# Layer norm 1 of two batches on a transposed copy of x, instead of TensorE transposes

## The chip, the cores and the metric

The kernel runs on one NeuronCore of one Trainium2 chip. The metric is the device time of one execution in microseconds, the median over runs. TensorE (PE) multiplies matrices into PSUM, VectorE (DVE) and ScalarE (ACT) work on SBUF and PSUM, GpSimd (POOL) on SBUF, and SyncE (SP) issues most of the DMAs. Each engine takes its instructions in the order in which the program emits them.

## The reference

One cross attention block with an MLP, in float32, for B = 4 batches of 512 rows of width D = 512, with 16 heads of 32 and an inner width of 2048:

```python
x = layer_norm(hidden_states, ln1_w, ln1_b)
q = (x @ q_w + q_b).reshape(B, LQ, H, HD).transpose(0, 2, 1, 3)
k = (encoder_hidden_states @ k_w + k_b).reshape(B, LK, H, HD).transpose(0, 2, 1, 3)
v = (encoder_hidden_states @ v_w + v_b).reshape(B, LK, H, HD).transpose(0, 2, 1, 3)
scores = jnp.where(mask, jnp.einsum('bhqd,bhkd->bhqk', q, k) * scale, mask_value)
out = jnp.einsum('bhqk,bhkd->bhqd', jax.nn.softmax(scores, axis=-1), v)
hidden = out.transpose(0, 2, 1, 3).reshape(B, LQ, D) @ cproj_w + cproj_b + residual
y = jax.nn.gelu(layer_norm(hidden, ln2_w, ln2_b) @ fc_w + fc_b, approximate=True)
return hidden + y @ proj_w + proj_b
```

Layer norm 1 is `(x - mean) * rsqrt(var + eps) * w + b`, with mean and variance over the width of each row, and `w` and `b` along the width.

## The kernel before, in words

The attention of the four batches is cut into 16 groups of four heads (`w`, four per batch), and each group into two halves of 256 queries. A half is a block `p`, from 0 to 31: batch 0 has blocks 0 to 7, batch 1 has 8 to 15, and so on. `block` emits, in this order: the scores of eight head and query tiles on PE (`scores`, line 260, eight PSUM banks, which is all there are), the softmax of the first four (`soften`: one DVE step, line 266, and one ACT exponential, line 270), two of the next four, two 32 by 32 block transposes on DVE (`turn`, line 278), the last two softmaxes, and two more `turn`. Between these steps `fill` runs other work, listed for each block by `put`: the products `prep_k`, `prep_q`, `prep_v` of a later group (k4 is the k product of group 4, and so on), output projections (`cproj`), MLP products (`fc_by_pair`, `proj`), loads and norms. `CHAIN` is a planned cost of one product, and `fill(0)`, `fill(1)` take items up to that cost, `fill(2)` the rest.

After a block its probabilities are exchanged between partitions: `copies` emits four POOL copies (line 335) and twelve DMAs on SP (line 340) into `pT`, of which there is one buffer (`gt` and `xe` serve for some blocks). `attend` (line 357) of a block comes two to three blocks later, ahead of the scores of the block it is due in, and its result is scaled on DVE into `oT` (line 362). PSUM tiles are taken in turn from eight banks, so a tile waits for whoever reads the tile eight places before it.

Layer norm 1 of a batch: x is loaded with rows on partitions into four tiles `xn`; DVE takes mean and variance (`ln_stat`, lines 127 and 128); POOL makes the reciprocal root (`ln_rs`, line 135); ACT or DVE normalises (`ln_norm`, lines 145 and 149); PE transposes 16 tiles of 128 by 128 through the identity into four PSUM tiles `tp` (`ln_turn`, line 158); ACT or DVE moves each to `xT` with weight and bias (lines 163 and 161). For batch 1 the norm stands at the end of block 0's fill (ACT), and the turns in block 4 (all moved by ACT). For batch 3 statistics stand in blocks 13 and 15, the norms (DVE) in 15, the turns in 16 and 17 (two moves by ACT, two by DVE). All batches share one `xT`, so the last q product of a batch must be done before the next batch's `xT` is written. Queries of batch 1 are first needed by q4 in block 5, those of batch 3 by q12 in block 18.

`xn` is a pool of four buffers that also holds the residual tiles `h` of batch 1's rows 256 to 511 and others. The first two residual tiles of batch 1 are in the pool `hids` (six buffers). In block 17 `load_h` loads residual tiles of batch 1, `c_bias` adds a row to each on POOL (line 368), and `cproj` (line 397) multiplies on PE and adds into them on DVE (line 398). `fc_sums` makes weight sums of the MLP on POOL (lines 469 and 472), and `y_sums` makes sums of the normed rows `yT` (tile `ys`), for batch 0 two on DVE and two on POOL, behind the k product of block 11.

Of the kernel before, what the change touches and what calls it, by code (L numbers as in the profile page):

```python
# [12 lines left out]
F32 = mybir.dt.float32  # L13
# [7 lines left out]
P = 128  # L21
# [16 lines left out]

BY_ACT = ((1, 1), (1, 2))
NORM_ACT = BY_ACT + ((2, 0), (2, 1))  # L40
# [9 lines left out]
@with_exitstack  # L50
def xattn_block(ctx: ExitStack, tc: tile.TileContext, x, encT, mask, q_w, k_w, v_w, c_w, fc_w, p_w, vecs, rows, out):
    nc = tc.nc
# [4 lines left out]

    const, keep, hids, tiles, small = pools(ctx, const=1, keep=1, hids=6, tiles=4, small=4)
    dram = ctx.enter_context(tc.tile_pool(name="dram", bufs=1, space=bass.MemoryType.DRAM))
# [9 lines left out]
    m8 = one.tile([P, L], U8, tag="m8", name="m8")  # L69
    nhalf = const.tile([P, NT], F32, tag="nhalf", name="nhalf")  # L70
    qb = const.tile([P, NG], F32, tag="qb", name="qb")
    wc = one.tile([P, ND, D], F32, tag="wc", name="wc")
# [57 lines left out]
    def ln_rs(key):  # L130

        ve = small.tile([P, NT], F32, tag="ve", name=f"ve{key[0]}_{key[1]}")
        nc.gpsimd.tensor_scalar(ve, S["mv", key][:, :, 1], EPS, 1.0, ALU.add, ALU.mult)
        rs = small.tile([P, NT], F32, tag="rs", name=f"rs{key[0]}_{key[1]}")
        nc.gpsimd.tensor_tensor(rs, ve, nhalf, ALU.pow)
# [143 lines left out]

    def block(w, half, fill, pairs):  # L280

# [88 lines left out]
    def stays(b, t):  # L370

        return b == 0 or b == SPLIT and t < 2

    def load_h(b, *ts_):

        if ("xa", b) not in S:
            S["xa", b] = dram.tile([L, D], F32, tag=f"xa{b}", name=f"xa{b}")
        for t in ts_:
            if b == B - 1:

                S["h", b, t] = k_q(t // 2, t % 2)
            else:
                pool, tag = (hids, "hid") if stays(b, t) else (tiles, "xn")
                S["h", b, t] = pool.tile([P, D], F32, tag=tag, name=f"h_{b}_{t}")
            Q[0].dma_start(out=S["h", b, t], in_=x[b, ts(t, P), :])
            if stays(b, t):
                S["hid", b, t] = S["h", b, t]
# [456 lines left out]
    def do(fn):  # L844
        return [(0.0, fn)]

    def A(w):
        if w >= NW:
# [32 lines left out]
    make_identity(nc, ident)  # L881
    nc.gpsimd.memset(nhalf, -0.5)
    load_enc(0)
    load_w(0, nc.sync, ("wv",))
# [17 lines left out]
    prep_k(1)  # L902
    run(turns1(0))
    load_h(0, *range(NT))
    nc.sync.dma_start(out=wc, in_=c_w)
# [7 lines left out]
    v_bias(0)  # L913

    def norm1(b, *ts_):
        for t in ts_:
            S["xn", b][t] = tiles.tile([P, D], F32, tag="xn", name=f"xn1_{b}_{t}")
            ln_norm((1, b), t, S["xn", b][t], gt[:, ts(t, D)])

    S["xn", 1] = [None] * NT  # L920
    x3 = turns1(1)


# [33 lines left out]

    ahead, fills = {}, {}

    def put(p, *work, before=()):  # L960

        work = [item for part in work for item in part]
        ahead[p] = list(before)
        fills[p] = work
# [22 lines left out]
    k, q, v = A(9)  # L987
    put(11, [k], do(lambda: y_sums(0)), [v], some(2), pb_(0))

# [33 lines left out]
    for p in range(2 * NW):  # L1023
# [10 lines left out]

        block(w, half, fill, any(cost > CHAIN for cost, _ in fills[p]))

# [61 lines left out]
```

## Time and profile before

| | us |
|---|---|
| median of 3 runs | 769.5 |
| lowest, highest | 768.61, 769.65 |
| the profiled execution | 768.29 |
| its span | 766.5 |

The span is from the first to the last instruction of the program; the rest of the profiled execution's time, 1.8 us, lies around it. The profile's page gives busy times by engine, the chain of work that ended last, and groups of instructions by source line; queries of the trace give timelines (start, length, engine, line, operation, operands, count, and in brackets the idle time before it and what ended it), waits, and busy time in chosen stretches. Times in timelines are microseconds from the start of the span. A float32 matmul stands as two records, a transpose as one. The recorded end of a matmul is modelled and overlaps the next start, so the cost of a matmul on PE is read from start to start.

### The profile page before, as it was taken

Reading aid. Unit: us, or ns where it says so; the run is one execution under the profiler, and the core shown is the slowest. Engines: PE = TensorE matmul, PEld = TensorE weight load, DVE = VectorE, ACT = ScalarE, POOL = GpSimd, SP = SyncE. Lnnn points to the kernel's source line nnn. Section 1 sums busy time; section 2 is a strip of 40 time slices with the busy share of each in tenths; the row PEclk is TensorE's granted clock in tenths of the full one; section 3 lists DMA queues with packets and bytes.
Section 4 is the critical chain, followed back from the end, with each engine's and each line's share of the span. In section 5 each row is a group of like instructions: output and inputs, shape, how many; then the busy total and the mean of one; then the engine's idle time right before and its main releaser. Section 6 shows DMA issues by size and latency. Waiting matters only on the chain.

```text
span 766.5 us, 13025 instructions
## 1 busy us (share of the span) xinstructions
PE 760.6 (99%) x4474; PEld 520.1 (68%) x4474; DVE 594.7 (78%) x1188; ACT 337.1 (44%) x761; POOL 312.6 (41%) x330
## 2 busy tenths in 40 slices
PE   9999999999999999999999999999999999999998
PEld 7656555566754745565554566447888889988997
DVE  3889899878989757887888989855777886747862
ACT  2676766564776444737753567501202221021200
POOL 1525447369466374234575444530060014303152
PEclk9999999999999999999999999999999999999999
DMA  9978788466866766675656866793724412146001
GB/s 330 319 223 228 180 209 253 117 196 193 254 196 189 189 208 180 163 185 130 173 128 190 214 197 193 173 296 132 262 101 129 162 34 90 35 131 219 2 15 42
DMA packets 58721, 131.44 MB, mean 171 GB/s; under 512 B 10992, under 2 KB 16752, under 8 KB 58528
## 3 DMA queue, kind: packets, MB, share of 16 engines
q1 hardware_dynamic: 56592, 123.58, 56.2%
q0 software_dynamic: 1920, 7.01, 2.7%
q8 instruction: 36, 0.59, 0.3%
q14 instruction: 29, 0.24, 0.1%
q10 hardware_dynamic: 144, 0.02, 0.0%
HBM read 66.08 MB, written 11.01 MB: 101 GB/s over the span
## 4 chain that ended last, share of the span: by engine, by line
PE 98%; DVE 1%; POOL 0%; ACT 0%; issue 0%; POOLq 0%
PE q L518 25%; PE accp L578 11%; PE r L665 8%; PE sc L260 8%; PE av L357 8%; PE accq L229 7%; PE accc L397 7%; PE accv L240 7%; PE acck L217 7%; PE q4p L701 2%; PE q1p L719 2%; PE tp L158 2%; PE warm L891 1%; DVE ptt L266 0%; PE q3p L701 0%; PE q5p L701 0%
## 5 line engine op out<-in xcount | busy, mean ns | idle before, releaser
L270 ACT ACTIVATE ptt<-ptt,mn 128x512 f32<-128x512 f32 x256 | 181.6, 711 | 148.6 <-DVE mn L266 148.6
L266 DVE CUSTOM_DVE_ANT_0 ptt<-sc,mb 128x512 f32<-128x512 f32 x256 | 160.5, 682 | 19.2 <-PE sc L260 19.2
L278 DVE STREAM_TRANSPOSE tb<-ptt 128x1024 f32<-128x1024 f32 x128 | 153.5, 1217 | 0.3 <-ACT ptt L270 0.2
L335 POOL COPY pT<-tb 32x1088 f32<-32x1088 f32 x96 | 105.2, 1096 | 38.1 <-DVE oT L362 14.4
L578 PE MATMUL accp<-pbt,gt 128*128 128x512 f32 x192 | 84.9, 596 | 0.0
L518 PE MATMUL q<-yT,gt 128*128 128x256 f32 x320 | 78.9, 380 | 0.0
L539 ACT ACTIVATE ga<-ga,vec 128x512 f32<-128x512 f32 x40 | 26.7, 714 | 92.0 <-DVE ga L472 92.0
L578 PEld LDWEIGHTS accp<-pbt,gt 128*128 128x128 f32 x192 | 35.9, 190 | 45.8 <-issue 39.3
L518 PEld LDWEIGHTS q<-yT,gt 128*128 128x128 f32 x320 | 60.9, 190 | 8.6 <-DMA xa<-pbt 0.2
L260 PE MATMUL sc<-pbt 32*128 32x512 f32 x512 | 64.7, 614 | 0.0
L240 PEld LDWEIGHTS accv<-ptt,xe 128*128 128x128 f32 x512 | 59.1, 192 | 7.4 <-DVE mn L266 4.9
L518 PE MATMUL q<-ys,gt 128*128 128x256 f32 x240 | 61.6, 380 | 0.0
L240 PE MATMUL accv<-ptt,xe 128*128 128x128 f32 x512 | 60.0, 276 | 0.0
L217 PE MATMUL acck<-xe,ptt 128*128 128x512 f32 x128 | 58.9, 603 | 0.0
L229 PE MATMUL accq<-xe,ptt 128*128 128x512 f32 (+1 forms) x136 | 58.3, 574 | 0.0
L397 PE MATMUL accc<-wc,oT 128*128 128x512 f32 x128 | 56.4, 597 | 0.0
L472 DVE TENSOR_TENSOR ga<-q,ga 128x512 f32<-128x512 f32 (+1 forms) x60 | 36.2, 603 | 21.4 <-PE q L518 19.4
L518 PEld LDWEIGHTS q<-ys,gt 128*128 128x128 f32 x240 | 45.7, 190 | 6.1
L270 ACT ACTIVATION_READ_ACCUMULATOR ptt<-ptt,mn 128x1 f32 x256 | 47.8, 187 | 0.0
L252 POOL TENSOR_TENSOR v<-v,row 128x512 f32<-128x512 f32 x16 | 20.4, 1280 | 64.7 <-ACT v L245 64.3
L357 PE MATMUL av<-pT,v 128*32 128x256 f32 x768 | 46.4, 382 | 0.0
L229 PEld LDWEIGHTS accq<-xe,ptt 128*128 128x128 f32 x136 | 25.1, 190 | 30.7 <-issue 23.1
(181 smaller groups left out, 1163.4 us busy)
## 6 DMA issues: line engine op xcount, KB each, us to landing
pT<-tb SPq DMA_DIRECT2D x288, 136.0 KB, 2.4
pbt<-p_w_dram SPq DMA_DIRECT2D x40, 256.0 KB, 3.3
gt<-ws SPq DMA_DIRECT2D x20, 512.0 KB, 3.4
gt<-tb SPq DMA_DIRECT2D x48, 136.0 KB, 2.4
xe<-tb SPq DMA_DIRECT2D x48, 136.0 KB, 2.4
pbt<-fc_w_dram SPq DMA_DIRECT2D x24, 256.0 KB, 4.1
gt<-fc_w_dram SPq DMA_DIRECT2D x20, 256.0 KB, 3.4
ptt<-k_w_dram SPq DMA_DIRECT2D x16, 256.0 KB, 3.7
```

The source lines that it names most:

```text
L217: nc.tensor.matmul(acc, S["wk", w][:, d, :], eT[:, d, :], start=(d == 0), stop=(d == ND - 1))
L229: nc.tensor.matmul(acc, S["wq", w][:, d, :], xT[:, d, c], start=(d == 0), stop=(d == ND - 1))
L240: nc.tensor.matmul(acc[:, ts(t, P)], eT[:, d, ts(t, P)], S["wv", w][:, d, :], start=(d == 0), stop=(d == ND - 1),)
L260: nc.tensor.matmul(S["sc", w, qt][h], qT[r, ts(qt, P)], kT[r, :], start=True, stop=True)
L266: nc.vector.tensor_tensor_reduce(out=s, in0=S["sc", w, qt][h], in1=S["mb", w // NG], scale=1.0, scalar=FMAX, op0=ALU.add, op1=ALU.min, acc ...
L270: nc.scalar.activation(s, s, AF.Exp, bias=mn, scale=-1.0, accum_out=S["sums", w][:, qt, h : h + 1])
L278: nc.vector.transpose(tv[:, qt % 2, 2 * k : 2 * k + 2], S["ps", w, qt, k])
L335: nc.gpsimd.tensor_copy(pT[ts(i, HD), i], tb[ts(i, HD), i])
L357: nc.tensor.matmul(av[ts(h, HD), : 2 * P].rearrange(shape, **kw), v[:, t, ts(h, HD)], p[t][h], start=(t == 0), stop=(t == NT - 1),)
L397: nc.tensor.matmul(acc, S["oT", b][:, g, ts(t, P)], wc[:, g, :], start=(g == 0), stop=(g == NG - 1))
L518: nc.tensor.matmul(o, x[:, k], y[:, k], start=(k == 0), stop=(k == 1))
L578: nc.tensor.matmul(acc, gT[q % 2][:, k, ts(t, P)], S["pw", b, q * FQ + k], start=(k == 0), stop=(k == FQ - 1))
```

## The change

For batches 1 and 3 the turns on PE go away. The host hands over a second copy of x, `rawT`, with the width on partitions. The statistics are still taken from x with rows on partitions. POOL writes `rs` and `-mean * rs` into a tile `rn`; DVE transposes `rn` in blocks of 32 by 32 (`store_rn`); four small DMAs on SP write it to DRAM as two rows of 512; two DMAs read each row back to all 128 partitions (`load_rn`). `load_raw` loads four 256 KB tiles of `rawT` into the `xn` buffers. POOL multiplies each by the first row and adds the second (`ln1_rows`, eight instructions of 128 by 512 for a batch); ACT applies weight and bias into `xT` (`ln1_affine`, four instructions).

The diff also changes the order around it. For batch 1, `load_raw` is issued behind batch 0's turns and ahead of `load_h`, `wc` and the MLP weights; `store_rn` stands in block 0, `load_rn` in block 1, the POOL work half in block 1 and half in block 2, `ln1_affine` at the end of block 4. For batch 3, `load_raw` and `store_rn` stand in block 15 ahead of four MLP weight loads and the exchange of block 15, `load_rn` and all eight POOL instructions in block 16 ahead of `fc_sums` and the copies of block 16, `ln1_affine` in block 17. The rows' two tiles take two of the six `hids` buffers (tag `hid2`), which batch 1's first two residual tiles share, so their load moves from block 16 to block 17. And all of `y_sums(0)` now runs on DVE, at a new place `mid` of block 11, between the first four softmaxes and the next two.

```diff
-BY_ACT = ((1, 1), (1, 2))
+BY_ROW = ((1, 1), (1, 3))
+BY_ACT = ((1, 2),)
...
+        if key in BY_ROW:
+            rs, nm = rn[:, :NT], rn[:, NT : 2 * NT]
+            nc.gpsimd.tensor_tensor(rs, ve, nhalf, ALU.pow)
+            nc.gpsimd.tensor_tensor(nm, S["mv", key][:, :, 0], rs, ALU.mult)
+            nc.gpsimd.tensor_scalar(nm, nm, -1.0, 0.0, ALU.mult, ALU.add)
+            return
...
+    def load_raw(b):
+        S["xn", b] = [tiles.tile([P, L], F32, tag="xn", name=f"raw_{b}_{d}") for d in range(ND)]
+        for d in range(ND):
+            nc.sync.dma_start(out=S["xn", b][d], in_=rawT[b, ts(d, P), :])
+
+    def store_rn(b):
+        nc.vector.transpose(rnT, rn)
+        d = S["rn", b] = dram.tile([2, L], F32, tag=f"rn{b}", name=f"rn{b}")
+        for i in range(NI):
+            nc.sync.dma_start(
+                out=d.rearrange("a (t i q) -> i (a t) q", i=NI, q=HD)[i], in_=rnT[i * HD : i * HD + 2 * NT, :]
+            )
+
+    def load_rn(b):
+        S["rows", b] = [hids.tile([P, L], F32, tag="hid2", bufs=2, name=f"rn_{b}_{i}") for i in range(2)]
+        for i in range(2):
+            nc.sync.dma_start(out=S["rows", b][i], in_=S["rn", b][i : i + 1, :].broadcast_to([P, L]))
+
+    def ln1_rows(b, *ds):
+        for d in ds:
+            for i, op in enumerate((ALU.mult, ALU.add)):
+                nc.gpsimd.tensor_tensor(S["xn", b][d], S["xn", b][d], S["rows", b][i], op)
+
+    def ln1_affine(b):
+        for d in range(ND):
+            nc.scalar.activation(
+                xT[:, d, :], S["xn", b][d], AF.Identity,
+                bias=vec[:, LN1B + d : LN1B + d + 1], scale=vec[:, LN1W + d : LN1W + d + 1],
+            )
...
         soften(w, q0, 0, 1, 2, 3)
+        run(mid)
         soften(w, q1, 0, 1)
...
-        e = nc.vector if b > SPLIT else nc.gpsimd
+        e = nc.gpsimd if b == SPLIT else nc.vector
...
-    put(0, [(CHAIN, lambda: prep_v(1)), v2, k2], do(lambda: norm1(1, *range(NT))))
-    put(1, [k3, (0.0, lambda: prep_q(1)), (CHAIN, lambda: (prep_v(3), load_enc(1)))])
-    put(2, [q2], [k4])
+    put(0, [(CHAIN, lambda: prep_v(1)), v2], do(lambda: store_rn(1)), [k2])
+    put(1, do(lambda: load_rn(1)), [k3, (0.0, lambda: prep_q(1)), (CHAIN, lambda: (prep_v(3), load_enc(1)))], do(lambda: ln1_rows(1, 0, 1)))
+    put(2, [q2], [k4], do(lambda: ln1_rows(1, 2, 3)))
     put(3, [q3, v4])
-    put(4, [k5], x3, [v5])
+    put(4, [k5, v5], do(lambda: ln1_affine(1)))
...
-    put(11, [k], do(lambda: y_sums(0)), [v], some(2), pb_(0))
+    put(11, [k, v], some(2), pb_(0), mid=do(lambda: y_sums(0)))
...
-    put(15, some(2), x2[1:2], some(1), x2[2:], some(1))
+    put(15, some(2), x2[1:2], do(lambda: load_raw(3)), some(1), do(lambda: store_rn(3)), some(1))
...
-    put(16, h_(1, 0, 1), [k, q], x3[:2], some(2), x3[2:3])
-    put(17, [v], x3[3:], h_(1, 2, 3), x4, cb(1), C(1))
+    put(16, do(lambda: load_rn(3)), [k], do(lambda: ln1_rows(3, *range(ND))), [q], some(2))
+    put(17, h_(1, 0, 1), [v], next_(lambda: ln1_affine(3)), h_(1, 2, 3), x4, cb(1), C(1))
```

More of the change, by code (lines that the diff above doesn't have):

```diff
@@ L50, in xattn_block @@
 @with_exitstack
-def xattn_block(ctx: ExitStack, tc: tile.TileContext, x, encT, mask, q_w, k_w, v_w, c_w, fc_w, p_w, vecs, rows, out):
+def xattn_block(ctx: ExitStack, tc: tile.TileContext, x, rawT, encT, mask, q_w, k_w, v_w, c_w, fc_w, p_w, vecs, rows, out):
     nc = tc.nc
@@ L56, in pools @@
         return [stack.enter_context(tc.tile_pool(name=n, bufs=k)) for n, k in bufs.items()]
-    const, keep, hids, tiles, small = pools(ctx, const=1, keep=1, hids=6, tiles=4, small=4)
+    const, keep, hids, tiles, small = pools(ctx, const=1, keep=1, hids=4, tiles=4, small=4)
     dram = ctx.enter_context(tc.tile_pool(name="dram", bufs=1, space=bass.MemoryType.DRAM))
@@ L70, in xattn_block @@
     nhalf = const.tile([P, NT], F32, tag="nhalf", name="nhalf")
+    rn, rnT = (const.tile([P, HD], F32, tag=n, name=n) for n in ("rn", "rnT"))
     qb = const.tile([P, NG], F32, tag="qb", name="qb")
@@ L278, in turn, with block @@
         nc.vector.transpose(tv[:, qt % 2, 2 * k : 2 * k + 2], S["ps", w, qt, k])
-    def block(w, half, fill, pairs):
+    def block(w, half, fill, pairs, mid):
         q0, q1 = 2 * half, 2 * half + 1
@@ L382, in load_h @@
             else:
-                pool, tag = (hids, "hid") if stays(b, t) else (tiles, "xn")
-                S["h", b, t] = pool.tile([P, D], F32, tag=tag, name=f"h_{b}_{t}")
+                pool, tag, n = (tiles, "xn", 4) if not stays(b, t) else (hids, "hid2", 2) if b else (hids, "hid", 4)
+                S["h", b, t] = pool.tile([P, D], F32, tag=tag, bufs=n, name=f"h_{b}_{t}")
             Q[0].dma_start(out=S["h", b, t], in_=x[b, ts(t, P), :])
@@ L845, in do, with next_ @@
         return [(0.0, fn)]
+    def next_(fn):
+        return [(0.01, fn)]
     def A(w):
@@ L882, in xattn_block @@
     nc.gpsimd.memset(nhalf, -0.5)
+    nc.gpsimd.memset(rn, 0.0)
     load_enc(0)
@@ L903, in xattn_block @@
     run(turns1(0))
+    load_raw(1)
     load_h(0, *range(NT))
@@ L913, in xattn_block @@
     v_bias(0)
[L915 to L921, printed above, removed]
     mlp = [
@@ L956, in norm, with put @@
         return do(lambda: [norm2(b, t) for t in ts_])
-    ahead, fills = {}, {}
-    def put(p, *work, before=()):
+    ahead, mids, fills = {}, {}, {}
+    def put(p, *work, before=(), mid=()):
         work = [item for part in work for item in part]
-        ahead[p] = list(before)
+        ahead[p], mids[p] = list(before), list(mid)
         fills[p] = work
@@ L1033, in fill @@
                 run(work, CHAIN if n < 2 else None)
-        block(w, half, fill, any(cost > CHAIN for cost, _ in fills[p]))
+        block(w, half, fill, any(cost > CHAIN for cost, _ in fills[p]), mids[p])
     gelus()
@@ L1074 @@
         "x": a["x"],
+        "rawT": np.ascontiguousarray(a["x"].transpose(0, 2, 1)),
         "encT": np.ascontiguousarray(a["ctx_2048"].transpose(0, 2, 1)),
```

## The prediction

> **What bounds the kernel now.** I read the page first, then the list of waits, then the timelines of each engine around the places that the change touches.
>
> ```profile
> span 766.5 us, 13025 instructions
> PE 760.6 (99%) x4474; PEld 520.1 (68%) x4474; DVE 594.7 (78%) x1188; ACT 337.1 (44%) x761; POOL 312.6 (41%) x330
> ...
> PE 98%; DVE 1%; POOL 0%; ACT 0%; issue 0%; POOLq 0%
> ```
>
> From the waits (us in total, times, longest), and from busy time in stretches of 20 us:
>
> ```profile
> DVE ptt L266 <- PE sc L260: 19.2, 30, 2.8
> ```
>
> ```profile
> 60.00:80.00 20.00, 20.00 (x156) 13.78 (x158) 19.06 (x43) 14.63 (x39) 8.22 (x8) 1.00 0.84 214
> ```
>
> PE is busy for 760.6 of 766.5 us and the chain that ended last lies 98% on PE. The wait row says the same from the other side: 30 of the 32 blocks begin with DVE waiting for PE's scores, so DVE has no backlog at a block's start. But it has little room either: in the stretch from 60 to 80 us, which holds batch 1's turns in block 4, DVE is busy for 19.06 of 20 us. So PE work that disappears is worth its own length, as long as nothing that PE waits for comes later than PE then arrives. The sum is a PE sum, and the question is what is late next.
>
> **What the change removes from PE.** The group of the turns, then PE's timeline in block 4 (batch 1) and in blocks 16 and 17 (batch 3):
>
> ```profile
> L158 PE MATMUL tp<-ident,xn 128*128 128x128 f32 x88 | 11.6, 273 | 0.0
> ```
>
> ```profile
> 74.11 1.91 PE L158 MATMUL tp<-ident,xn 128*128 128x128 f32 x16
> 75.85 3.74 PE L240 MATMUL accv<-ptt,xe 128*128 128x128 f32 x32
> ```
>
> ```profile
> 252.05 1.04 PE L158 MATMUL tp<-ident,xn 128*128 128x128 f32 x8
> 252.92 1.89 PE L518 MATMUL q<-yT,pbt 128*128 128x256 f32 x8
> ...
> 258.96 0.60 PE L158 MATMUL tp<-ident,xn 128*128 128x128 f32 x4
> 259.50 1.93 PE L357 MATMUL av<-pT,v 128*32 128x256 f32 x32
> ...
> 266.96 0.60 PE L158 MATMUL tp<-ident,xn 128*128 128x128 f32 x4
> 267.40 13.90 PE L397 MATMUL accc<-wc,oT 128*128 128x512 f32 x32
> ```
>
> From start to start, batch 1's sixteen turns hold PE for 75.85 - 74.11 = 1.74 us. Batch 3's come in three pieces: 0.87 + 0.54 + 0.44 = 1.85 us. Together 3.59 us, or 0.11 us for each of the 32. The group's row gives 273 ns as the mean of one; that is a duration that overlaps the next start, so I use the starts. [...]
>
> The turns' moves and norms go from ACT and DVE, and four ACT steps of similar form per batch come (`ln1_affine`). In block 4 they stand on ACT where the four moves stood, so q4 in block 5 sees them no later than now; in block 17 they stand behind the MLP's gelu, a block ahead of q12. I cost both at nothing; if q12 or q4 had to wait, it would be by a step, under 1 us. DVE gains one transpose of 128 by 32 per batch, an eighth as wide as the smallest of each block's, in block 0 and in place of four norms in block 15; nothing.
>
> **What the move of `y_sums(0)` is worth.** Block 11 has the largest stall of PE in the attention; the same MLP step a block later shows the undisturbed spacing (timelines of PE, DVE and POOL):
>
> ```profile
> 173.83 1.03 PE L518 MATMUL q<-ys,wsum 128*128 128x256 f32 x4
> 175.93 1.13 PE L518 MATMUL q<-yT,pbt 128*128 128x256 f32 x4 [1.07 <-POOL yT L469]
> ...
> 188.64 1.03 PE L518 MATMUL q<-ys,wsum 128*128 128x256 f32 x4
> 189.50 1.03 PE L518 MATMUL q<-yT,pbt 128*128 128x256 f32 x4
> ```
>
> ```profile
> 171.38 0.69 DVE L469 TENSOR_TENSOR ys<-yT 128x512 f32<-128x512 f32 x1
> 172.10 1.46 DVE L469 TENSOR_TENSOR ys<-yT,ys 128x512 f32<-128x512 f32 x1
> ...
> 181.64 0.42 DVE L362 TENSOR_TENSOR oT<-av,pT 128x256 f32<-128x256 f32 x1 [1.26 <-PE av L357]
> ```
>
> ```profile
> 174.61 1.27 POOL L469 TENSOR_TENSOR yT<-yT 128x512 f32<-128x512 f32 x1
> ```
>
> 175.93 - 173.83 = 2.10 us against 189.50 - 188.64 = 0.86: PE loses 1.24 us, and the bracket names the POOL half of `y_sums(0)`, which starts at 174.61 because POOL has its copies first. On DVE the four sums are about 2.9 us (1.46 for two). In their new place they come ahead of four softmax steps and two turns that stand before 171.38 now, so even with the two more they end before the 173.6 at which the DVE half ends now. PE waits for them no more. The stall goes: -1.24 us. In exchange DVE carries 1.4 us more in this block and the block is 1.24 us shorter. The row at 181.64 shows 1.26 us of waiting for PE, and other waits of the block (1.1 us for the stalled product) go with the stall; what is left covers it by about 1 us. If POOL's sums, which run at the same time, held up DVE's, that 1 us goes first.
>
> **What is late next, batch 3.** This is the term on which I spend most. The rows of the way from the norm's factors to block 18, on SP, among the DMA issues, on POOL and on DVE:
>
> ```profile
> 238.80 2.90 SPq L461 DMA_DIRECT2D pbt<-p_w_dram  x4
> 244.03 7.50 SPq L340 DMA_DIRECT2D pT<-tb  x12
> 251.58 1.07 SPq L385 DMA_DIRECT2D h<-x_dram  x2
> ```
>
> ```profile
> h<-x_dram SPq DMA_DIRECT2D x12, 256.0 KB, 4.4
> ```
>
> ```profile
> 261.98 0.72 POOL L472 TENSOR_TENSOR wsum<-pbt 128x256 f32<-128x256 f32 x1 [12.93 <-DMA pbt<-fc_w_dram]
> ...
> 271.32 1.26 POOL L252 TENSOR_TENSOR v<-v,row 128x512 f32<-128x512 f32 x1 [0.44 <-ACT v L245]
> 272.55 2.49 POOL L368 TENSOR_TENSOR h<-h,row 128x512 f32<-128x512 f32 x2
> 275.41 2.50 POOL L368 TENSOR_TENSOR h<-h,row 128x512 f32<-128x512 f32 x2 [0.37 <-DMA h<-x_dram]
> ```
>
> ```profile
> 240.79 1.92 DVE L149 TENSOR_SCALAR xn<-xn,mv,rs 128x512 f32<-128x512 f32 x4 [0.94 <-POOL rs L135]
> ...
> 281.41 0.69 DVE L398 TENSOR_TENSOR h<-accc,h 128x512 f32<-128x512 f32 x1 [2.74 <-PE accc L397]
> 283.23 0.42 DVE L362 TENSOR_TENSOR oT<-av,pT 128x256 f32<-128x256 f32 x1 [1.13 <-PE av L357]
> 284.25 0.69 DVE L266 CUSTOM_DVE_ANT_0 ptt<-sc,mb 128x512 f32<-128x512 f32 x1 [0.60 <-PE sc L260]
> ```
>
> I follow it on the clock of before. The factors are ready when DVE's norms start now, 240.79, or a little later (two more short POOL steps): say 241.5 for the transpose. Behind it on SP wait four row stores, then the four weight loads of L461, and then the exchange of block 15, which starts at 244.03 now. At 0.47 us an issue (1.85 us for four, row 47.27 below) the eight end at 245.2, and the twelve exchange issues (7.50 us) at 252.8; PE reads that exchange only at 259.50. Then come the two row loads, in the place of the two `h` loads of 251.58. With the 4.4 us that such loads take to land, the second lands near 257.7.
>
> Then POOL: eight instructions at 2.49/2 = 1.25 us (L368 has the same form), of which the first overlaps the second load's landing: until about 267.5. Behind them wait the weight sums of `fc_sums`, which start at 261.98 now, the copies of block 16, the bias of v, and `c_bias` for four residual tiles. From 261.98 to 272.55 is 10.57, less the 0.44 of waiting in row 271.32 is 10.1 us; four tiles are 5.0 us. So the last tile is ready at 267.5 + 10.1 + 5.0 = 282.6, against 277.9 now (275.41 + 2.50). Its sum on DVE (0.69) and the scaling of `oT` (0.42, pipelined to 0.35) follow, and the first softmax of block 18 can start near 283.7.
>
> Now it starts at 284.25; with batch 3's turns gone, PE would be there 1.85 us earlier, at 282.4. (The 2.98 us saved in blocks 4 and 11 move both sides alike.) So DVE starts 1.3 us late, all eight PSUM banks are taken by scores, and PE loses 1.3 us. Bounds: if the row loads land as fast as the exchange's and the eight start 2 us earlier, nothing; if each of the eight costs 0.36 us more, as in the dearest POOL group of the trace (below), 1.3 + 2.9 = 4.2 us. I take 1.3, since L368 is the same operation on the same shape.
>
> ```profile
> L469 POOL TENSOR_TENSOR ga<-gs,ga 128x512 f32<-128x512 f32 x4 | 6.4, 1611 | 4.1 <-DVE ga L469 4.1
> ```
>
> **What is late next, batch 1.** `load_raw` adds 1 MB and the row loads 0.5 MB to a busy time, and SP issues ten more DMAs ahead of batch 1's encoder load (SP, the DMA issues with KB and median us to landing, PE, and a stretch, whose last two columns are the DMA share and GB/s):
>
> ```profile
> 47.27 1.85 SPq L171 DMA_DIRECT2D xe<-encT_dram  x4
> ```
>
> ```profile
> xe<-encT_dram SPq DMA_DIRECT2D x16, 256.0 KB, 4.9
> ```
>
> ```profile
> 52.25 3.60 PE L217 MATMUL acck<-xe,ptt 128*128 128x512 f32 x8
> ```
>
> ```profile
> 46.00:48.00 2.00, 2.00 (x20) 1.56 (x22) 0.05 (x1) 0.58 (x1) 0.38 (x1) 1.00 0.03 11
> ```
>
> k4 starts at 52.25 and takes its four pieces 0.9 us apart, the last near 54.9. The last is issued near 48.7 and lands about 4.9 us later, 53.6: a slack of about 1 us. The DMAs rest almost fully from 46 to 48 (share 0.03), and the 1.5 MB are 6 us of full share (60 to 80 us moved 214 GB/s at a share of 0.84); most of it has been worked off by then in gaps ahead or fits there. I take 0.2 us, bounds 0 and 2.
>
> POOL's two halves for batch 1 (5 us each) come ahead of the copies of blocks 1 and 2, which are needed two blocks later; nothing, and with that cover gone, up to 5 us.
>
> **Sum.** -1.74 - 1.85 - 1.24 + 1.3 + 0.2 = -3.3 us. The profiled execution took 768.29 us (span 766.5 and 1.8 around it), so it would become 765.0. The median of the runs, 769.5, is 1.2 us above it; 769.5 - 3.3 = 766.2 us is the forecast. About 0.2%, 1.5 us, is what a measurement of this kernel can tell from no change.
>
> **The rivals.**
>
> *All of the gain.* The row loads land early, block 18 starts on time: -4.8 us, 764.7. For it: POOL idles for 12.9 us ahead of 261.98, and the rows could start there. Against it: SP's order, which puts them behind twelve exchange issues. Chance 0.20.
>
> *The opening.* The extra 1.5 MB delays the encoder load and k4 waits by 2 us: 1.8 us more than in the sum, -1.5, 768.0. For it: slack of only 1 us. Against it: the idle stretch at 46 to 48. It also stands for a dearer POOL in block 16. Chance 0.14.
>
> *Slower: each of POOL's eight instructions in block 16 first waits for a DVE instruction.* Then each costs 0.69 us more, 5.5 us in all; block 18's first softmax starts 6.8 us late, and the kernel is at -3.3 + 5.5 = +2.2 us, 771.7. It decides from 0.42 us per instruction on (3.3/8). Against it, the bias of v in block 3, one of POOL's sums of the same shape, in the stretch in which DVE was busy for 19.06 of 20 us:
>
> ```profile
> 68.48 1.27 POOL L252 TENSOR_TENSOR v<-v,row 128x512 f32<-128x512 f32 x1 [5.73 <-ACT v L245]
> ```
>
> It took 1.27 us. Chance 0.05. [...]
>
> *The transposes free what one lasts.* Were it 273 ns of PE for each of the 32 and not 0.11 us, the gain would be 8.7 + 1.24 - 1.5, 761.0. The starts speak against it. [...]
>
> **How the numbers follow.** Forecast 0.60, 764.9 to 767.6 by the bounds of its terms; all of the gain 0.20; opening or dearer POOL 0.14; slower 0.05; the rest 0.01. The range from 764.4 to 768.7 leaves out a little of the second case and most of the fourth and the dear end of the third, between 1 and 2 in 10. Faster by over 0.2% (below 768.0): 0.60 + 0.20 + 0.01 and a little of the third, 0.83. Within: 0.11. Slower: 0.06.
>
> **What would show it.** In the profile after: no `tp` turns of batches 1 and 3, block 4 (from its first score to that of block 5) 1.74 us shorter; no POOL wait of PE in block 11; POOL's eight steps of block 16 at 1.25 us each, starting some 15 us after the block's scores; the fourth residual sum of block 17 as the last thing ahead of block 18's softmax, with PE waiting about 1 us there. The forecast is wrong if k4 waits for the encoder, if `fc_sums` or the copies of block 16 come late enough to stop an `attend`, or if DVE loses more than 1 us in block 11.

## The result, and the profile after

| | before | after |
|---|---|---|
| median, us | 769.05 (11 runs, 767.78 to 770.17) | 772.31 (11 runs, 768.55 to 774.27) |
| ratio to before | | 1.0041, 95% interval 1.0025 to 1.0058 |
| profiled execution, its span, us | 768.29, 766.5 | 771.84, 770.0 |

The change is slower by 3.3 us. The forecast, 766.2 with a range to 768.7, was wrong in sign. The page after: span, busy time by engine, and the chain that ended last by engine.

```profile
span 770.0 us, 13012 instructions
PE 761.1 (99%) x4442; PEld 516.6 (67%) x4442; DVE 592.7 (77%) x1186; ACT 336.0 (44%) x759; POOL 329.5 (43%) x347
PE 95%; POOL 2%; DMA 1%; DVE 1%; ACT 1%; issue 0%; SPq 0%; POOLq 0%
```

PE's share of the chain fell from 98% to 95%: POOL, DMAs and ACT now have pieces of it. PE's recorded busy time is not less than before although 32 transposes are gone, because the record of a product that waits for its accumulator counts as busy: the scores of block 18, which wait, stand without a gap at 4.48 us instead of 2.00 (below). So I compare lengths, from the first score of a block to the first of the next (us; a dash: as before to 0.1):

| block | before | after | what changed in it |
|---|---|---|---|
| opening to block 0 | 21.52 | 22.22 | the first k product, 4.42 us from start to start for 3.71; 20.9 to 22.2 in all the profiles |
| 2 | 10.86 | 15.73 | k4 waits |
| 4 | 12.74 | 10.99 | batch 1's turns gone |
| 11, 12 | 18.38, 13.47 | 17.04, 13.94 | `y_sums(0)` |
| 16, 17 | 18.22, 21.73 | 16.90, 21.30 | batch 3's turns gone |
| 18 | 16.90 | 19.38 | softmax late |
| others | | - | |

The gains are there, -1.75, -1.34 and -1.75 us, and block 12 gives 0.47 back; blocks 2 and 18 lose 4.87 and 2.48. With 0.70 in the opening and -0.2 in small differences elsewhere, that makes the +3.5 us between the spans.

**Block 2.** PE's timeline after (start, length, engine, line; in brackets the idle time before and what ended it):

```profile
49.42 3.70 PE L267 MATMUL accq<-xe,ptt 128*128 128x512 f32 x8
56.29 2.29 PE L255 MATMUL acck<-xe,ptt 128*128 128x512 f32 x4 [3.17 <-DVE mn L304]
59.06 2.36 PE L255 MATMUL acck<-xe,ptt 128*128 128x512 f32 x4 [0.48 <-DMA xe<-encT_dram]
```

Before, k4 (`acck`) followed q2 without a gap at 52.25. Now PE stands idle 3.17 us and then 0.48 more for the next pieces of `xe`, the encoder rows of batch 1. The first bracket names DVE, but in the trace the first piece of `xe` lands at 56.20, 0.09 us before the product starts; the second bracket names the transfer itself. Why it lands late is read on SP's queue (`SPq`: DMA issues; the length of a group contains SP's waits):

```profile
18.39 1.75 SPq L200 DMA_DIRECT2D raw<-rawT_dram  x4
23.78 8.39 SPq L500 DMA_DIRECT2D pbt<-fc_w_dram  x8
34.60 2.25 SPq L206 DMA_DIRECT2D rn<-rnT  x4
37.24 8.98 SPq L379 DMA_DIRECT2D pT<-tb  x12
46.92 0.89 SPq L213 DMA_DIRECT2D rn<-rn  x2
49.66 2.64 SPq L179 DMA_DIRECT2D xe<-encT_dram  x4
```

and in the stretch that was the rest of the DMAs (last two figures: DMA share, GB/s):

```profile
46.00:48.00 2.00, 2.00 (x19) 1.69 (x21) 0.19 (x1) 0.40 (x1) 0.00 (x0) 1.00 0.85 217
```

Four raw loads stand at 18.39, four stores of the rows at 34.60, two row loads at 46.92. The first exchange starts at 37.24 instead of 32.62 (the row of before, below), and the encoder load at 49.66 instead of 47.27. The share from 46 to 48 is 0.85, not 0.03: the rest that I counted on was used up by work that had been pushed into it.

```profile
32.62 8.47 SPq L340 DMA_DIRECT2D pT<-tb  x12
```

The trace also shows how added bytes hold up the queue itself: many DMAs are issued just after the landing of the DMA eight issues ahead of them. The second, third and fourth issue of the exchange come at 37.91, 38.54 and 39.44, each 0.02 us behind such a landing.

**Block 18.** POOL, SP, DVE and PE after:

```profile
246.79 4.47 POOL L374 COPY pT<-tb 32x1088 f32<-32x1088 f32 x4 [0.38 <-DMA rn<-rnT]
261.07 10.39 POOL L218 TENSOR_TENSOR raw<-raw,rn 128x512 f32<-128x512 f32 x8 [9.82 <-DMA rn<-rn]
271.42 0.73 POOL L511 TENSOR_TENSOR wsum<-pbt 128x256 f32<-128x256 f32 x1
275.86 4.49 POOL L374 COPY pT<-tb 32x1088 f32<-32x1088 f32 x4
280.43 1.26 POOL L290 TENSOR_TENSOR v<-v,row 128x512 f32<-128x512 f32 x1
281.66 4.95 POOL L407 TENSOR_TENSOR h<-h,row 128x512 f32<-128x512 f32 x4
```

```profile
244.60 1.30 SPq L206 DMA_DIRECT2D rn<-rnT  x4
247.88 9.34 SPq L379 DMA_DIRECT2D pT<-tb  x12
257.26 1.08 SPq L213 DMA_DIRECT2D rn<-rn  x2
```

```profile
282.95 0.69 DVE L437 TENSOR_TENSOR h<-accc,h 128x512 f32<-128x512 f32 x1 [8.82 <-POOL h L407]
286.64 0.69 DVE L437 TENSOR_TENSOR h<-accc,h 128x512 f32<-128x512 f32 x1 [0.53 <-POOL h L407]
287.58 0.68 DVE L304 CUSTOM_DVE_ANT_0 ptt<-sc,mb 128x512 f32<-128x512 f32 x1
```

```profile
284.35 4.48 PE L298 MATMUL sc<-pbt 32*128 32x512 f32 x16
288.77 3.70 PE L267 MATMUL accq<-xe,ptt 128*128 128x512 f32 x8
```

This is the chain of the forecast, row by row: the exchange (9.34 us for twelve), row loads at 257.26, POOL idle for 9.82 us until one lands, eight steps at 10.39/8 = 1.30 us, `fc_sums`, copies, the bias, four residual rows, four residual sums, and only then the first softmax, at 287.58. The scores take 4.48 us instead of 2.00, as each of the later ones waits for an accumulator.

The exchange took 9.34 us and not 7.50 because SP waited in it, three times, for landings of the weight loads `p_w` that stand eight issues ahead; before, no issue of this exchange waited for a DMA:

```profile
SPq L379 <- DMA pbt<-p_w_dram: 1.9, 3, 1.0
```

**Blocks 11 and 12.** PE after, in the MLP step of block 11 and ahead of block 13:

```profile
175.98 1.89 PE L557 MATMUL q<-yT,pbt 128*128 128x256 f32 x8
177.71 1.03 PE L557 MATMUL q<-ys,wsum 128*128 128x256 f32 x4
...
196.06 1.93 PE L396 MATMUL av<-pT,v 128*32 128x256 f32 x32 [0.40 <-POOL pT L374]
```

```profile
180.96 1.27 POOL L290 TENSOR_TENSOR v<-v,row 128x512 f32<-128x512 f32 x1 [2.81 <-ACT v L283]
```

The products of block 11 follow each other without a gap. The 0.40 us at 196.06 is new: `attend` waits for POOL's copies of an exchange, and POOL is late since its bias of v waited 2.81 us for ACT, whose exponentials now stand behind DVE's four sums at `mid`.

### The profile page after: what moved, and what is told of

Its sections match the earlier page's. It is cut to its first block, busy times and chain, and to the rows that moved or that the text cites. A ratio compares the mean times of both kernels' runs of the same rounds, so it can differ in the third digit from the quotient of the medians.

```text
span 770.0 us, 13012 instructions
## 1 busy us (share of the span) xinstructions
PE 761.1 (99%) x4442; PEld 516.6 (67%) x4442; DVE 592.7 (77%) x1186; ACT 336.0 (44%) x759; POOL 329.5 (43%) x347
## 4 chain that ended last, share of the span: by engine, by line
PE 95%; POOL 2%; DMA 1%; DVE 1%; ACT 1%; issue 0%; SPq 0%; POOLq 0%
PE q L557 25%; PE accp L617 11%; PE r L704 8%; PE sc L298 8%; PE av L396 8%; PE acck L255 7%; PE accv L278 7%; PE accq L267 7%; PE accc L436 5%; PE q4p L740 2%; PE q1p L758 2%; PE tp L166 1%; DMA xe<-encT_dram 1%; POOL pT L374 1%; POOL h L407 1%; DVE ptt L304 1%
## 5 line engine op out<-in xcount | busy, mean ns | idle before, releaser
L298 PE MATMUL sc<-pbt 32*128 32x512 f32 x512 | 67.1, 615 | 0.1
L255 PE MATMUL acck<-xe,ptt 128*128 128x512 f32 x128 | 60.5, 612 | 3.8 <-DVE mn L304 3.2
L255 PEld LDWEIGHTS acck<-xe,ptt 128*128 128x128 f32 x128 | 23.4, 194 | 36.8 <-issue 21.8
```

The lines of the kernel that those rows point to most:

```text
L255: nc.tensor.matmul(acc, S["wk", w][:, d, :], eT[:, d, :], start=(d == 0), stop=(d == ND - 1))
L298: nc.tensor.matmul(S["sc", w, qt][h], qT[r, ts(qt, P)], kT[r, :], start=True, stop=True)
```

## The experiments

All times are medians against the kernel before in the same session (768.55 to 769.04). Where one batch keeps its turns, four PSUM tiles are taken in passing at the end of the attention, so that later products find the same banks. The diffs are shortened to the lines that matter.

**1 to 3: one part alone.** Batch 1 by rows; batch 3 by rows; only the move of `y_sums(0)` (which experiments 1 and 2 hold too). The edits are the two lists and, for the batch that keeps its turns, the `put` lines of before:

```diff
-BY_ROW = ((1, 1), (1, 3))
+BY_ROW = ((1, 1),)      # experiment 1;  ((1, 3),) in 2, () in 3
```

> Batch 1 by rows as in the change, batch 3 by turns on TensorE as before, y_sums(0) on VectorE. Theory A (the DMAs added to the opening delay the encoder load of batch 1, and k4 in block 2 waits): block 2 is again about 15.7 us long instead of 10.86 (+4.9), block 4 1.75 us shorter, blocks 11 and 12 together 0.9 us shorter, blocks 16 to 18 as before; in all about +2.3 us against the kernel before. Theory B (the loss comes from GpSimd's queue in blocks 16 to 18, and the wait in block 2 was an accident of one execution): block 2 at about 10.9, in all about -2.6 us.

> Batch 3 by rows as in the change, batch 1 by turns as before, y_sums(0) on VectorE. Theory A: block 2 at 10.86 us, blocks 16 and 17 together 1.75 us shorter, block 18 2.5 us longer (19.4), blocks 11 and 12 0.9 shorter; in all about -0.2 us against before. Theory B: block 18 loses more than the half of the whole loss, in all +2 us or more.

> Both batches by turns as before; only y_sums(0) is moved to VectorE and to its new place in block 11. Block 11 goes from 18.4 to 17.0 us and block 12 from 13.5 to 13.9, since the bias of v and the copies on GpSimd come later behind ScalarE's copy of v: in all -0.9 us. If the wait of block 12 in the profile after was an accident: -1.3 us.

| | median (runs) | ratio, interval | block 2 | 4 | 11+12 | 16+17 | 18 |
|---|---|---|---|---|---|---|---|
| batch 1 | 769.58 (12) | 1.0011 [1.0000, 1.0022] | 13.85 | 10.99 | 30.97 | 39.95 | 16.90 |
| batch 3 | 771.95 (6) | 1.0048 [1.0034, 1.0061] | 10.86 | 12.74 | 30.98 | 38.39 | 21.62 |
| `y_sums` | 767.73 (11) | 0.9988 [0.9979, 0.9996] | 10.86 | 12.74 | 30.97 | 39.95 | 16.90 |

(Before, blocks 11 and 12 sum to 31.85, 16 and 17 to 39.95.) The move of `y_sums(0)` is a gain of 1.1 us by the times. Batch 1 alone loses 2.99 us in block 2: the wait that theory A speaks of, but less than its 4.9, and the time is +0.8 us against its +2.3 (and B's -2.6). Batch 3 alone was to be neutral by A and is 3.1 us slower, which is on B's side: block 18 loses 4.7 us, 2.2 more than in the changed kernel's profile. PE in block 18 of that kernel, and two stretches of 3.41 us there (the last three figures of such a row are the granted clock, the DMA share and GB/s):

```profile
280.92 5.02 PE L298 MATMUL sc<-pbt 32*128 32x512 f32 x16
285.87 5.40 PE L267 MATMUL accq<-xe,ptt 128*128 128x512 f32 x8
```

```profile
282.54:285.95 3.41, 3.21 (x9) 0.96 (x7) 2.88 (x8) 0.54 (x1) 2.88 (x4) 1.00 0.24 93
285.95:289.36 3.41, 3.41 (x4) 1.38 (x5) 3.41 (x11) 3.41 (x11) 3.29 (x4) 0.50 0.98 276
```

The scores wait about as they did, but the q product behind them takes 5.40 us instead of 3.70: the granted clock is 0.50 from 285.95 to 289.36. That was in neither theory.

**4: both loads of batch 1 later.** The four raw and the two row loads behind the encoder load, the POOL steps a block later:

```diff
-(prep_v(3), load_enc(1))
+(prep_v(3), load_enc(1), load_rn(1), load_raw(1))
```

> The changed kernel, but for batch 1 the two row loads and the four loads of transposed x are issued right behind the encoder load of batch 1 in block 1, and GpSimd's two halves stand in blocks 2 and 3 instead of 1 and 2. Theory A: block 2 back at 10.9 us, block 4 still 11.0, block 18 still 19.4; in all about 4.9 us below the changed kernel, -1.7 us against before. If SyncE's wait for the row stores alone, which stay in block 0, is the cause: block 2 still several us longer.

774.03 us (6 runs), 1.0081 [1.0065, 1.0097]: 5.2 us over before, where 1.7 us under it was expected. Block 2 is 10.86, so what stands ahead of the encoder load is what delayed it. But block 4 is 17.85 and block 3 11.68. DVE and PE there:

```profile
66.71 2.37 DVE L316 STREAM_TRANSPOSE tb<-ptt 128x1024 f32<-128x1024 f32 x2 [4.79 <-POOL pT L374]
```

```profile
75.33 5.85 PE L255 MATMUL acck<-xe,ptt 128*128 128x512 f32 x8
```

The exchange of block 1 now stood behind six loads. `tb` has two buffers, so block 3's first turn waited 4.79 us for it; then the clock was 0.50 for 6.83 us from 72.87. The loads were moved from in front of one transfer that is just in time to in front of another.

**5 to 8: each half mended.** Batch 3's preparation earlier (alone; batch 1 by turns); fc_w's first loads out of the opening (batch 1 alone); both together; and only the order of the opening changed:

```diff
-put(15, ... do(lambda: load_raw(3)), some(1), do(lambda: store_rn(3)), some(1))
-put(16, do(lambda: load_rn(3)), [k], ...
+put(15, do(lambda: (load_raw(3), store_rn(3))), some(2), some(1), do(lambda: load_rn(3)), some(1))
+put(16, [k], ...
```

```diff
-    load_mlp()                                   # opening
+put(4, [k5], do(lambda: load_mlp(4)), ...        # and two each in blocks 5 and 6
```

> Batch 1 by turns as before; batch 3 by rows, but all of its preparation earlier: the four residual statistics and the power in block 13, the raw loads and the row stores at the start of block 15, the broadcast loads before block 15's last projection; GpSimd's eight steps stay in block 16. Theory A (block 18 lost because GpSimd's chain started too late, and its start hung on the chain statistics, transpose, stores, exchange, broadcast loads): GpSimd starts the eight steps some 15 us earlier, block 18 is back at 16.9, blocks 16 and 17 keep their -1.75, block 11 and 12 keep -0.9 together; in all -2.6 us, 766.2. Rival B (the chain of eight steps on GpSimd itself, or its place before the value bias, is what costs): block 18 stays over 18.5, and the time is 768.0 or more.

> Batch 3 by turns as before; batch 1 by rows as in the change, but the first eight loads of fc_w (2 MB), which nothing reads before block 10, are issued in blocks 4 (four), 5 (two) and 6 (two) instead of in the opening. Theory A (SP's queue and the DMA engines are full in the opening, the 1 MB of raw x and the row loads push the encoder load of batch 1 back, and TensorE waits for it in block 2): with 2 MB less ahead of them block 2 is 10.9 to 11.5, block 4 keeps its -1.75, the y sums their -0.9; in all -2.0 to -2.7 us, 766.1 to 766.8. Rival B (the row loads and stores beside the encoder load, or the wait of the raw loads for TensorE's turns, cost it, not the bytes ahead): block 2 stays over 13 us, and the time is 768.5 or more.

> The change with both moves: the first eight loads of fc_w in blocks 4 to 6, and batch 3's preparation in blocks 13 and 15. If both theories A hold, the gains add up: -1.75 (block 4), -1.75 (blocks 16 and 17), -0.9 (blocks 11 and 12), none lost in blocks 2 and 18: -4.4 us, 764.4. If one of the two B holds, 766 to 767; if both, 769 or more.

> The change, with the four loads of raw x for batch 1 moved from ahead of the residual, c_w and fc_w loads to behind the fc_w loads, all else as in the change: the same bytes on the same queue, only in another order, and without the wait for TensorE's turns in front of 3 MB of loads. Theory A (bytes and issues ahead of the encoder load): block 2 stays long, 13 to 16 us. Rival B (the wait for the turns in front of the other loads): block 2 is 10.9 to 11.5.

| | median (runs) | ratio, interval | block 2 | 14 | 16 | 17 | 18 |
|---|---|---|---|---|---|---|---|
| batch 3 early | 765.94 (5) | 0.9969 [0.9957, 0.9981] | 10.86 | 13.47 | 16.90 | 21.30 | 16.95 |
| fc_w late, batch 1 | 767.05 (11) | 0.9978 [0.9969, 0.9987] | 12.41 | 13.49 | 18.23 | 21.73 | 16.90 |
| both | 765.73 (6) | 0.9965 [0.9953, 0.9978] | 11.07 | 13.86 | 17.65 | 21.30 | 16.95 |
| raw loads behind fc_w | 773.13 (1 run) | | 13.50 | 13.49 | 17.20 | 21.30 | 23.35 |

Batch 3 is settled: with its POOL steps from 247.62 on the loss of block 18 is gone and the gain of 1.75 stays.

```profile
247.62 10.37 POOL L218 TENSOR_TENSOR raw<-raw,rn 128x512 f32<-128x512 f32 x8
```

```profile
280.57 2.00 PE L298 MATMUL sc<-pbt 32*128 32x512 f32 x16
282.58 3.67 PE L267 MATMUL accq<-xe,ptt 128*128 128x512 f32 x8
```

For batch 1, 2 MB less ahead take block 2 from 13.85 to 12.41, not to 10.9: theory A is right in direction and leaves something over. The mere order of the loads does not mend it (13.50, in one execution). "Both" fell short of -4.4 by block 2 and by 1.1 us in blocks 14 and 16, where PE stood idle ahead of an `attend`; I did not follow those two up, and all but 0.1 us of them is gone in the next version.

**9 to 11: a lighter opening, and the clock.** The residual loads of batch 0 moved to block 4 as well, fc_w spread over blocks 5, 6, 7 and 9, batch 3's raw loads and stores moved to block 14; and two kernels with filler products on PE, one for block 18 (batch 3 alone), one for block 2 (batch 1 alone):

```diff
-put(14, [q], some(2))
+put(14, [q], some(2), do(lambda: (load_raw(3), store_rn(3))))
```

```diff
+ for i in range(2): matmul(sc[h], zero, kT[r, :], start=False, stop=i == 1)   # block 18, each score
+ for i in range(6): matmul(acc, ident, S["kT", 2], start=True, stop=True)     # ahead of k4
```

> The change with a lighter opening and an earlier batch 3: the residual loads of batch 0 (1 MB) go to block 4, the first eight loads of fc_w to blocks 5, 6, 7 and 9 (two each); batch 3's statistics all in block 13, its raw loads and row stores at the end of block 14, its broadcast loads at the start of block 15. Theory A (bytes and issues ahead of the encoder load of batch 1 are what block 2 loses, a late start is what block 18 loses): block 2 is 10.9 to 11.1, block 14 13.5, block 16 16.9, block 18 16.9 to 17.0; in all -1.75 -1.75 -0.9 = -4.4 us, 764.2, and runs closer together than the 3.4 us of the version with fc_w alone moved. Rival B (another wait of the row path is left): block 2 over 11.5 or a loss of over 0.5 in blocks 4 to 9, and 765.5 or more.

> Batch 3 alone by rows, as in the second experiment, where block 18 took 21.6 us and the granted clock was 0.5 for 3.4 us from the end of its drawn-out scores. Behind each of the block's eight score products two further products with zero weights are added into the same accumulator (adding zero), so that TensorE works through the stretch in which it waits for accumulators. Theory A (the clock is halved because TensorE did too little in the 3.4 us before): the granted clock stays 1.0 there, block 18 is 19.4 to 20.0, the median falls from 771.95 to 769.5 to 770.5. Rival B (the clock falls for another reason): 0.5 again and block 18 at 21.6 or more, median 772 or more.

> Batch 1 alone by rows, as in the first experiment (769.58 median, 767.16 to 771.7), with six products of 128x512 (some 2.8 us) on TensorE ahead of the key projection of head group 4, in the stretch where it waits 2.7 us for the encoder load; their result is overwritten. Theory A (the spread of that kernel's times comes from clock halvings that this wait sets off in some executions): the runs draw together below 770 and the median falls to 769.0 or less. Rival B (the spread comes from when the transfers land): median and spread stay, 769.6 and some 4 us, or rise by at most 0.5 where the encoder comes early.

The lighter opening: 765.67 us (5 runs, 764.95 to 766.57), 0.9964 [0.9950, 0.9977]. Blocks 14, 16 and 18 are 13.57, 16.90 and 16.95, as A said. Block 2 is 12.43, as B said, with another 1 MB gone. PE there:

```profile
54.88 2.34 PE L255 MATMUL acck<-xe,ptt 128*128 128x512 f32 x4 [0.60 <-DMA xe<-encT_dram]
```

Both filler kernels were mis-sized by me. The sixteen zero products took 0.4 us each, one after the other, and the scores with them 9.55 us instead of 5.02; the kernel is at 774.00 us. The clock, though, stayed at 1.0, and the q product behind took 3.70 us. The six products ahead of k4 took 5.31 us, not 2.8; block 2 was 16.01 and the time 771.27. Its runs lay within 0.9 us (770.66 to 771.58) instead of 4.5: with the wait covered, the spread was gone too. The clock and the landing both have a part in it: the mean granted clock on record is 0.998 in five of the twelve executions of experiment 1 (median 770.9 us) and 1.000 in the other seven (median 768.9, still 2.9 us apart), and 1.000 in all five with the filler.

**12 to 14: what stands right ahead of the encoder load; a filler that fits; the lighter opening alone.**

```diff
-put(1, do(lambda: load_rn(1)), [k3, ...
+put(2, do(lambda: load_rn(1)), [q2], [k4])       # and the POOL steps in blocks 3 and 4
```

> As the version with the light opening, but the two broadcast loads of batch 1's rows (0.5 MB), which stood in front of the encoder load, are issued in block 2 behind the exchange of block 1; GpSimd's steps go to blocks 3 and 4. Theory A (in block 2 TensorE still waits because the row loads stand right in front of the encoder load): block 2 is 10.9, blocks 3 to 5 stay at 11.0, 11.0, 10.9; 764.2, with a spread of 1 us or less. Rival B (the encoder load itself lands that late, with no row load in front of it): block 2 between 11 and 12.5 in some executions, the spread 1.5 us or more, 765 or more. Rival C (the row loads delay the exchange of blocks 1 and 2, as in the fourth experiment): block 2 is 10.9 and block 3 or 4 longer by 0.5 or more.

> Batch 3 alone by rows, with one product with zero weights behind each of the last four score products of block 18 only (0.4 us each by the last filler experiment, where sixteen of them ran one after the other and took 4.5 us more than the scores' wait). Theory A (the clock is halved because TensorE does too little while it waits for accumulators): the clock stays 1.0 from 280 to 296 us, the first key or query product behind the scores takes 3.7 us, block 18 is 19.4 to 20.0, the median 769.5 to 770.5. Rival B: the clock falls to 0.5, that product takes 5 us or more, block 18 is 21.6, the median 772.

> The kernel before, with only the residual loads of batch 0 and the first eight loads of fc_w moved out of the opening, as in the version with the light opening. Theory A (the kernel before has its cover of some 1 us for the encoder load only in some executions, and its own spread of 2 us is that load): the runs draw together at the lower end, median 768.0 to 768.3, block 2 at 10.9. Rival B (the encoder load is covered in every execution of the kernel before): median and spread unchanged, 768.7 and 2 us.

The row loads behind block 1's exchange: 764.71 us (5 runs, 763.73 to 765.09), ratio 0.9945 [0.9933, 0.9957], the fastest of all, 4.3 us under before, with a spread of 1.4 us. Block 2 is 10.86, and blocks 3, 4, 5 are 11.00, 11.00, 10.90. PE and POOL:

```profile
52.53 3.60 PE L255 MATMUL acck<-xe,ptt 128*128 128x512 f32 x8
```

```profile
63.11 5.25 POOL L218 TENSOR_TENSOR raw<-raw,rn 128x512 f32<-128x512 f32 x4
74.47 5.23 POOL L218 TENSOR_TENSOR raw<-raw,rn 128x512 f32<-128x512 f32 x4
```

The rows of the encoder load on SP, in this order: the change, raw loads behind fc_w, fc_w late, lighter opening, rows late. Beside them block 2: 15.73, 13.50, 12.41, 12.43, 10.86.

```profile
49.66 2.64 SPq L179 DMA_DIRECT2D xe<-encT_dram  x4
47.99 1.88 SPq L179 DMA_DIRECT2D xe<-encT_dram  x4
47.74 1.84 SPq L179 DMA_DIRECT2D xe<-encT_dram  x4
47.07 1.85 SPq L179 DMA_DIRECT2D xe<-encT_dram  x4
47.55 1.85 SPq L179 DMA_DIRECT2D xe<-encT_dram  x4
```

The openings differ in length, so I take these times from the first score of block 2: 2.17, 1.31, 0.49, 0.48 and 0.49 us, and 0.48 in the kernel before. The issue was late in the first two only. With the third and the fourth it was as early as before, and the load still cost 1.6 us; with the fifth, where the row loads no longer stand ahead of it, it cost nothing, and the five executions of the fourth and of the fifth, each set against its own session's kernel before, do not overlap (medians 3.0 and 4.3 us under it). This points to the row loads, which in the first four are issued 2.7 to 4.5 us ahead of the encoder load (46.92 and 49.66 in the change, 42.58 and 47.07 in the fourth), but does not single them out. The fifth also moved POOL steps. The version of experiment 7, with the row loads ahead and the encoder load issued at 47.10 (0.48 us again), lost only 0.2 us in its profile. And in the two filler kernels for block 18, in which batch 1 has its turns and no row loads, block 2 was 12.35 and 11.07 with the issue at 0.48: the cover of the encoder load is not sure in every execution.

The lighter opening on the kernel before: 768.83 (12 runs), 1.0001 [0.9992, 1.0009]. It is worth nothing by itself, so the 4.3 us belong to the change and its placing. Its spread of 2.2 us stayed, so a fuller opening is not what spreads the times of the kernel before.

The filler for the last four scores gave 772.21 (7 runs, 769.53 to 774.95), and the clock fell. Stretches of that kernel:

```profile
281.24:284.65 3.41, 3.30 (x13) 1.35 (x10) 2.14 (x4) 0.00 (x0) 3.13 (x4) 1.00 0.03 10
284.65:288.06 3.41, 3.41 (x10) 2.14 (x8) 3.41 (x12) 2.51 (x7) 3.09 (x4) 0.50 0.83 276
288.06:291.48 3.42, 3.42 (x6) 1.26 (x5) 3.42 (x7) 1.83 (x6) 1.81 (x2) 0.50 0.95 224
```

The first filler was issued only at 283.15, in the second half of the stretch ahead of the fall. Rival B by the numbers of this profile, but the filler came too late in it to test A. The seven executions differ: the mean granted clock on record is 0.999 or 1.000 in four of them (769.53 to 772.21 us) and 0.993 to 0.996 in three (772.76 to 774.95). Without a filler (experiment 2) it is 0.995 or 0.998 in all six, and with sixteen zero products (experiment 10) 1.000 in all four.

## Why the prediction was wrong

**What the change removes: right.** Batch 1 -1.75 (said: -1.74), batch 3 -1.75 (said: -1.85), the wait in block 11 -1.34 (said: -1.24). Transposes counted from start to start, not by 273 ns, are what PE gained.

**`y_sums(0)`: nearly.** I looked for what the move costs only on DVE in its own block, and found cover. The cost came over ACT and POOL, 0.47 us in block 12, by the way that the prediction's last lines name: copies late enough to stop an `attend`. The trade is -0.9 by the blocks and -1.1 by the times.

**"What is late next, batch 1" failed, and it decides the sign.** I took 0.2 us with bounds 0 and 2; it was 4.87 in the profile of the change and 2.99 in experiment 1. I worked out that the 1.5 MB would be worked off in gaps ahead or in the rest of the DMAs at 46 to 48, and kept the landing at 53.6. I did not carry ten issues and 1.5 MB through SP's queue step by step, as I did for batch 3. It was named as a rival ("the opening"), but with a bound of 2 us for which no row stood; even with both upper bounds, 4.2 and 2, the sum would have been only +1.4 us. What the runs showed in its place: taken from the block's first score, the first piece of the load is issued at 2.17 instead of 0.48 us and takes 6.54 instead of 3.45 us to land, against a cover of about 1 us. The late issue needs the bytes ahead of it (2 MB less, and it is early again); the last 1.5 us point to the row loads, but their cause stays open. The rest in the table of shares was cover for this load, not free room.

**"What is late next, batch 3": right mechanism, mis-sized.** 1.3 us said, with bounds 0 and 4.2; 2.48 in the profile after. The prediction worked on the clock of before; ahead of block 13 the changed kernel is 2.95 us behind it (0.70 + 4.87 - 1.75 - 1.34 + 0.47), so I take that off its times. The transpose and the eight issues came as said (issues until 244.8, said 245.2). The step that was mis-sized is the next one, the exchange at its old length: 9.34 us and not 7.50, for SP's 1.9 us of waiting for the weight loads, so that it ended at 254.3 and not 252.8. The POOL steps ended at 268.5 (said 267.5), and the 0.9 us stayed in the chain to the first softmax, 284.6 (said 283.7). The other 0.25 us: the block loses 0.35 more than the softmax is late, for a reason that no run isolates, and 0.10 less since the turns gave 1.75 and not 1.85. The DVE rival did not come: 1.30 us a step, against 1.27 for the bias of v.

**What was not in the prediction at all: a PE wait can cost twice.** In the sixteen profiles of this study the granted clock is 1.00 or 0.50, and each stretch of 0.50 inside a kernel lasts 3.41 or 6.83 us: in block 18 of experiments 2, 8 and 13, and in blocks 4 and 18 of experiment 4. The change's own profile has none. Within a profile the stretches begin a whole number of such lengths apart (experiment 2: 285.95, and 770.65 at the end of the run; the 484.70 us between are 142 times 3.413), so I take them as edges of a fixed grid. In experiment 2 the grid stretch ahead of the fall, 282.54 to 285.95, holds nine records of PE, of the scores mainly: an estimate of 1.1 us of work at the undisturbed 2.00/16 us a record, the rest waiting. In the change's own profile the drawn-out scores share their grid stretch (283.81 to 287.22) with the end of an `attend`, 24 records, and the clock held. On the grid of the change's profile the wait of block 2 falls into two pieces, and the clock held; at the end of experiment 4 it fell at 772.60:

```profile
51.70:55.11 3.41, 1.42 (x4) 0.35 (x2) 3.41 (x7) 2.03 (x6) 3.30 (x3) 1.00 1.03 307
55.11:58.52 3.41, 2.16 (x4) 0.59 (x4) 3.41 (x8) 2.38 (x6) 3.32 (x3) 1.00 1.06 265
```

```profile
769.19:772.60 3.41, 1.31 (x7) 0.81 (x5) 0.43 (x1) 0.00 (x0) 0.00 (x0) 1.00 0.11 38
```

So the clock fell after 1.31 us of PE work in 3.41, and held after 1.42. The single executions on record bear out that a wait brings the fall in some executions and not in others. One such stretch takes 0.5 x 3.41/770 = 0.002 off an execution's mean clock. For the change the mean is 1.000 in four of eleven executions (770.62 to 771.97 us) and 0.995 to 0.998 in seven, six of which took 772.31 to 774.27. It is 0.998 or less in five of twelve of experiment 1, and never in the kernel before (69 executions beside the experiments) nor in the versions whose profiles lose at most 1.6 us in block 2 and no more than 0.1 in block 18 (55 executions). So the falls are a part of the change's spread of 5.7 us, not all of it: its fastest execution, 768.55, has 0.997. The spread of before, 2.4 us, has another cause. That the place of the grid decides is argued: no run moved it. The fillers speak for the work as the cause: the clock fell in none of nine executions in which they cover the wait (experiments 10 and 11), against eleven of eighteen of the same two kernels without. A single idle gap did not always bring the fall: the clock held through one of 3.17 us (block 2 of the change), and fell after stretches that held about a third of their work (1.31 of 3.41 us in experiment 4, an estimated 1.1 in experiment 2).

## What to carry to other kernels

Work taken off the busiest engine was worth its start-to-start length here (1.75 us in block 4, for 1.74 on PE before), and the change had that right; its price was in the order of the queue. Follow every DMA that an edit adds through its queue to the next transfer that lands just in time, on both sides of where it is put, and place it behind that transfer and ahead of the one after; the same edit was worth +3.3 us or -4.3 us by nothing but where loads, and the steps on them, were put. And price a wait of the matrix engine above its length, with the chance of a halved clock behind it (1.70 us more for one q product here).

## What was not expected of the hardware

The halved clock after a stretch with about a third of its PE work (1.31 of 3.41 us in experiment 4), for 3.41 or 6.83 us, at a price of 1.70 us for one q product (5.40 against 3.70). Zero products behind scores ran one after the other at 0.4 us each (9.55 us for 24), while the scores alone, on four groups of 32 rows, took 0.25 us each (2.00 us for eight). What makes the difference no run shows.
